# A perceiver block with a mixture of experts on one core: the gates get a tile of their own, the small groups' PSUM banks trade places, and three groups' folds move to the end

## The chip, the core and the metric

The kernel runs on one core of one Trainium2 chip. The metric is device time in microseconds; of several runs the median counts. The engines are named as in the profile: PE (TensorE's matmuls) and PEld (its weight loads), DVE (VectorE), ACT (ScalarE), POOL (GpSimd) and SP (SyncE, here the queue that issues the weights' DMAs). A `q` behind a name stands for the engine's sequencer, which waits, branches and issues.

## The reference

Three layers act on x, 8 x 64 tokens of 512 numbers, in float32: cross attention over a context of 8 x 1601 rows, a causal linear attention with a dense MLP, and a mixture of eight experts. The change lies in the third:

```python
router_logits = x @ w_router                       # x: the 512 normalized tokens
top_w, top_i = jax.lax.top_k(router_logits, K)     # K = 2
top_w = jax.nn.softmax(top_w)
gating = jnp.zeros((t, e)).at[jnp.arange(t)[:, None], top_i].add(top_w)
for ei in range(e):                                # 8 experts
    hmid = jax.nn.silu(x @ w0[ei]) * (x @ w1[ei])  # 512 -> 1024
    out = out + gating[:, ei:ei + 1] * (hmid @ wo[ei])
```

The result is added to the input of the layer.

## The kernel before

**Stages.** The span goes through cross attention (to about 164 us), linear attention (its first products begin at 129), the MLP (from 287), the routing (about 380 to 411 us) and the experts (411 us to the end). All weights come through one ring of 12 tiles that SP fills in a fixed order (`stream`, `need`, L117 to L208), six tiles ahead; a tile is issued when the matmuls that used its place are done. The order of each engine's instructions is the order of the program (a manual schedule, L95); semaphores are set by the framework from the tiles that instructions touch.

**Routing.** For each of four tiles of 128 tokens the kernel normalizes the rows into `mn` (L868, 512 columns of values and 8 of gates for each tile), writes the rows to a table in DRAM, `mn_dram` (`write`, L901), picks two experts for each token (`choose`, L933) and ranks the tokens of each expert (`rank_tile`, `tabulate`). The gates are computed last (L1102 to L1114) straight into `mn[:, :, D:]`, and a DMA on ACT's queue copies them to the last 8 columns of `mn_dram` (L1115). Then `banks.close()` and `mid.close()` (L1121, L1122) give back the PSUM banks and the SBUF pools of the middle of the kernel, `mn`'s among them (`mlp`, L814). The new pools, `pse` for PSUM and `moe2` for SBUF, are laid over them. The pool `moe` (L101) stays open from beginning to end.

**PSUM in the experts' stage.** Eight banks: three "side 0" banks and one y bank for whole tiles, two "side 1" banks (`side_bank(1)`) and one y bank (`y_bank(1)`) for the branches, one for transposed rows.

**An expert.** `whole_tile` (L1215) handles the first 128 tokens of an expert: four `up` products of 512 columns (L1224), Silu on ACT and a product on DVE (`gated`, L1182), transposes (`hidden_t`, L1189), and `down` products into y (L1232). `add_rows` (L1197) multiplies y by the gate into y_sb, on ACT (L1204) or, with `by_vector`, on DVE (L1202), and POOL adds the rows to `out` with an indirect DMA (L1205). Between its parts a whole tile turns the rows of the next expert (`turn_tile`, L1162; rows of a small group go through a side 1 bank).

Tokens beyond 128 are handled in branches that are taken or skipped at run time (`few_tokens`, L1549): up to 32 more tokens by `group` (L1254), up to 96 by `three_groups` (L1318). The test for `three_groups` (L1551) stands ahead of the one for `group` (L1553). A skipped branch still adjusts each engine's semaphore to the count that the branch would have left. In this input the experts 0, 3 and 5 take `group`, expert 2 takes `three_groups`, and 1, 4, 6 and 7 take neither (L1550; for 6 and 7 one test at L1595).

`group` lays four slices of 32 columns of the array side by side: its `up` (L1278) makes two halves h, each followed by Silu (L1286) and product (L1288); `turn` (L1265) transposes a half and copies it out, on DVE for the first and on ACT for the second; `down` (L1291) sums into two banks; two copies (L1310) and a product with `fold` (L1313) add the four slices. `three_groups` does the same for three groups of 32 tokens in full width: `up` (L1332), `turn` (L1346), `down` (L1353) with the copies L1366 to L1369, and `folded` (L1371). Their order is written out by hand at L1378 to L1391. The experts end with the whole tile of expert 7, its y_sb and its scatter.

Of the kernel before, what the change touches and what calls it, by code (L numbers as in the profile page):

```python
# [15 lines left out]
F32 = mybir.dt.float32  # L16
AF = mybir.ActivationFunctionType
ALU = mybir.AluOpType
# [29 lines left out]
def perceiver_kernel(  # L48
# [816 lines left out]

    mn = mlp.tile([P, NT, D + NE], F32, tag="mn", name="mn")  # L868
    full = [P, NT, NE]
    rank = moe.tile(full, F32, name="rank")  # L870
    spot = moe.tile([P, NT, 2], mybir.dt.uint32, name="spot")
# [18 lines left out]
    def finish(t):  # L890

        nc.vector.tensor_tensor(xs[:, t, :], acc[t], xs[:, t, :], ALU.add)  # L892
        st = small.tile([P, 6], F32, tag="st", name=f"st_m_{t}")
        nc.vector.bn_stats(st, xs[:, t, :])
        mv, rstd = moments(t, st)
        nc.vector.tensor_scalar(
            mn[:, t, :D], xs[:, t, :], mv[:, 0:1], rstd, ALU.subtract, ALU.mult
        )
        write(t)

    def write(t):  # L901
        nc.scalar.dma_start(mn_dram[t * P : (t + 1) * P, :D], mn[:, t, :D])
        nc.gpsimd.dma_start(out[t * P : (t + 1) * P, :], xs[:, t, :])

    def last_chunks(t, part):
# [171 lines left out]
    nc.vector.bn_stats(st[:, 1, :], xs[:, t, halves[1]])  # L1077
    mv, rstd = moments(t, st)
    nc.vector.scalar_tensor_tensor(neg_mean, mv[:, 0:1], -1.0, rstd, ALU.mult, ALU.mult)
    nc.scalar.activation(mn[:, t, :D], xs[:, t, :], AF.Identity, bias=neg_mean, scale=rstd)  # L1080
    first_rows(2)
    logits_of(t, range(2, KC))
    choose(t)
# [23 lines left out]
    nc.vector.tensor_scalar_add(r1, e2, 1.0)  # L1107
    nc.vector.reciprocal(r1, r1)
    nc.vector.tensor_tensor(e2, e2, r1, ALU.mult)
    gating = mn[:, :, D:]  # L1110
    nc.vector.tensor_tensor(gating, hot[:, :, 0, :], r1[:, :, None].to_broadcast(full), ALU.mult)
    hot2g = moe.tile(full, F32, name="hot2g")
    nc.vector.tensor_tensor(hot2g, hot[:, :, 1, :], e2[:, :, None].to_broadcast(full), ALU.mult)
# [11 lines left out]
    if True:  # L1125
# [71 lines left out]
        def add_rows(key, y, n, side, by_vector=False):  # L1197

            _, dst, gate = slots[key]
            y_sb = moe2.tile([P, D], F32, tag=f"ysb{side}", bufs=2 - side, name=f"y_sb_{key[0]}_{key[1]}")  # L1200
            if by_vector:
                nc.vector.tensor_scalar(y_sb[:n, :], y[:n, :], gate[:n, :], None, ALU.mult)  # L1202
            else:
                nc.scalar.activation(y_sb[:n, :], y[:n, :], AF.Copy, scale=gate[:n, :])  # L1204
            nc.gpsimd.indirect_dma_start(  # L1205
                out=out,
                out_offset=bass.IndirectOffsetOnAxis(ap=dst[:n, :], axis=0),
                in_=y_sb[:n, :],
                in_offset=None,
                bounds_check=B * S + P - 1,  # L1210
                oob_is_err=True,
                compute_op=ALU.add,
            )
# [40 lines left out]
        def group(e, up_of, down_of):  # L1254


            nm = f"{e}_1"
            xg_t = turned[e, 1]


            split = "p (w n) -> p w n"
            halves = [slice(h * P, (h + 1) * P) for h in range(2)]
            hid, h_t = [], {}

            def turn(j):  # L1265
                bank = side_bank(1, f"ht_{nm}_1") if j else y_bank(1, f"ht_{nm}_0")
                nc.tensor.transpose(bank[:, :P], hid[j], ident)
                h_t[j] = moe2.tile([P, P], F32, tag="hidT1", name=f"hidT_{nm}_{j}")
                (nc.scalar.copy if j else nc.vector.tensor_copy)(h_t[j], bank[:, :P])

            for h in range(2):
                bank = side_bank(1, f"up_{nm}_{h}")
                for c in range(KC):

                    if h == 1 and c == KC - 1:
                        turn(0)
                    for q in range(NQ):
                        nc.tensor.matmul(  # L1278
                            bank[q * R : (q + 1) * R, : 2 * P].rearrange(split, w=2),
                            xg_t[c],  # L1280
                            up_of[q][:, c, :].rearrange(split, w=2)[:, :, halves[h]],
                            start=(c == 0),
                            stop=(c == KC - 1),
                        )
                act = moe2.tile([P, P], F32, tag="act1", name=f"act_{nm}_{h}")
                nc.scalar.activation(act, bank[:, :P], AF.Silu)  # L1286
                hid.append(moe2.tile([P, P], F32, tag="mid1", name=f"mid_{nm}_{h}"))
                nc.vector.tensor_tensor(hid[h], bank[:, P : 2 * P], act, ALU.mult)  # L1288
            sums = {}

            def down(j, n):  # L1291
                if j == 0:
                    sums[n] = y_bank(1, f"yq_{nm}_1") if n else side_bank(1, f"yq_{nm}_0")
                for q in range(NQ):
                    nc.tensor.matmul(
                        sums[n][q * R : (q + 1) * R, : D // 2],
                        h_t[j][:, q * R : (q + 1) * R],
                        down_of[q // 2][:, 2 * (q % 2) + j, n * D // 2 : (n + 1) * D // 2],
                        start=(j == 0),
                        stop=(j == 1),  # L1300
                    )

            down(0, 0)
            turn(1)
            down(0, 1)
            parts = []
            for n in range(2):
                down(1, n)
                parts.append(moe2.tile([P, D // 2], F32, tag="parts", name=f"parts_{nm}_{n}"))
                (nc.scalar.copy if n else nc.vector.tensor_copy)(parts[n], sums[n][:, : D // 2])  # L1310
            y = side_bank(1, f"y_{nm}")
            for n in range(2):
                nc.tensor.matmul(  # L1313
                    y[:R, n * D // 2 : (n + 1) * D // 2], fold, parts[n], start=True, stop=True
                )
            add_rows((e, 1), y, R, 1)

        def three_groups(e, up_of, down_of):  # L1318
# [32 lines left out]
                nc.vector.tensor_copy(h_t[g].rearrange("p j q -> p (j q)"), bank[:, : 2 * P])  # L1351

            def down(g):  # L1353
                bank = side_bank(1, f"yq_{nm}_{g}")
                for j in range(2):
                    for q in range(NQ):
                        nc.tensor.matmul(
# [3 lines left out]
                            start=(j == 0),  # L1361
                            stop=(j == 1),
                        )
                parts[g] = moe2.tile([P, D], F32, tag="parts3", name=f"parts_{nm}_{g}")
                if g < 2:
                    nc.scalar.copy(parts[g], bank)  # L1366
                else:
                    nc.vector.tensor_copy(parts[g][:, : D // 2], bank[:, : D // 2])
                    nc.scalar.copy(parts[g][:, D // 2 :], bank[:, D // 2 :])  # L1369

            def folded(g):  # L1371
                for n in range(2):
                    cols = slice(n * D // 2, (n + 1) * D // 2)
                    nc.tensor.matmul(
                        y[g * R : (g + 1) * R, cols], fold, parts[g][:, cols], start=True, stop=True
                    )

            up(0)  # L1378
            up(1)
# [1 line left out]
            up(2)  # L1381
            turn(1)
            down(0)
            down(1)
            turn(2)
            y = side_bank(1, f"y3_{nm}")
            folded(0)
            down(2)
            folded(1)
            folded(2)  # L1390
            add_rows((e, 1), y, REST, 1, by_vector=True)  # L1391

        if True:
# [313 lines left out]
```

## Time and profile before

| | us |
|---|---|
| three runs | 652.44, 654.95, 656.95 |
| median | 654.95 |
| the profiled execution: its own time | 652.34 |
| its span, first to last instruction | 650.2 |
| routing ends, expert 0's first `up` | 411.07 |
| `group` of expert 0 | 436.19 to 443.90 |
| `three_groups` of expert 2 | 489.98 to 510.87 |
| `group` of expert 3 | 534.73 to 542.44 |
| `group` of expert 5 | 589.02 to 596.74 |
| last y_sb, last scatter issued | 641.79, 642.76 |

The mean granted clock of TensorE is 0.995 of full speed. The page gives the busy time and share of each engine, the chain of work that ended last, and the costliest groups of instructions; a group's line names source line, engine, operation, output and inputs, shape and count. In an answer in order of time, a line gives start and duration in us, and in brackets how long the engine stood idle before it and what ended that. A list of waits gives who waited, for whom, us in total, times and the longest.

### The profile page before, as it was taken

Reading aid. Unit: us, or ns where it says so; the run is one execution under the profiler, and the core shown is the slowest. Engines: PE = TensorE matmul, PEld = TensorE weight load, DVE = VectorE, ACT = ScalarE, POOL = GpSimd, SP = SyncE. Lnnn points to the kernel's source line nnn. Section 1 sums busy time; section 2 is a strip of 40 time slices with the busy share of each in tenths; the row PEclk is TensorE's granted clock in tenths of the full one; section 3 lists DMA queues with packets and bytes.
Section 4 is the critical chain, followed back from the end, with each engine's and each line's share of the span. In section 5 each row is a group of like instructions: output and inputs, shape, how many; then the busy total and the mean of one; then the engine's idle time right before and its main releaser. Section 6 shows DMA issues by size and latency. Waiting matters only on the chain.

```text
span 650.2 us, 7530 instructions
## 1 busy us (share of the span) xinstructions
PE 622.0 (96%) x2956; PEld 293.3 (45%) x2956; DVE 180.8 (28%) x438; ACT 128.6 (20%) x246; POOL 62.1 (10%) x82
## 2 busy tenths in 40 slices
PE   4999999999999999999999999899999999999994
PEld 3743535343444444455444457544443444443442
DVE  4011333232316878660000035411311101011110
ACT  2241222220132123031101201311111111111110
POOL 3000000000000000050000002250102002103000
PEclk9999999999999999999999999999999999999998
DMA  8999999999521203030311222339392549496611
GB/s 325 417 423 422 424 425 422 427 426 423 219 98 34 98 1 131 1 130 0 129 64 67 81 98 106 108 94 349 123 368 46 199 204 306 185 367 191 282 18 16
DMA packets 23860, 133.99 MB, mean 206 GB/s; under 512 B 4080, under 2 KB 4080, under 8 KB 12288
## 3 DMA queue, kind: packets, MB, share of 16 engines
q1 hardware_dynamic: 19456, 124.64, 48.0%
q0 software_dynamic: 3248, 7.58, 5.3%
q10 hardware_dynamic: 1104, 1.07, 0.5%
q8 instruction: 34, 0.56, 0.3%
q14 instruction: 18, 0.15, 0.1%
HBM read 128.37 MB, written 4.91 MB: 205 GB/s over the span
## 4 chain that ended last, share of the span: by engine, by line
PE 47%; DMA 25%; issue 22%; DVE 2%; POOL 1%; POOLq 1%; ACT 0%; SPq 0%; DVEq 0%; ACTq 0%
DMA out_dram<-y_sb,dst_late 11%; DMA ctx<-in_ctx_dram 10%; PE hid L823 8%; PE mlp L844 7%; PE wk L631 4%; PE wq L631 4%; PE v L551 4%; PE wo L742 4%; PE pw L374 3%; DMA ctxT<-in_ctx_T_dram 2%; PE av L487 2%; PE sc L429 2%; PE pr_wq L647 1%; PE xo L521 1%; PE qk L673 1%
## 5 line engine op out<-in xcount | busy, mean ns | idle before, releaser
L1224 PE MATMUL up<-e_up,xgT 128*128 128x512 f32 x224 | 100.2, 595 | 2.1 <-ACTq L1550 0.8
L1224 PEld LDWEIGHTS up<-e_up,xgT 128*128 128x128 f32 x224 | 40.9, 190 | 49.7 <-issue 48.2
L1232 PE MATMUL y<-e_wo,hidT 128*128 128x512 f32 x128 | 60.7, 598 | 0.0
L823 PE MATMUL hid<-v_sb,w 128*128 128x512 f32 (+2 forms) x144 | 56.6, 545 | 0.0
L1186 DVE TENSOR_TENSOR mid<-up,act 128x256 f32<-128x256 f32 x35 | 14.8, 425 | 134.6 <-ACT act L1184 134.6
L844 PE MATMUL mlp<-w,hid_sb 128*128 128x512 f32 x112 | 51.0, 597 | 0.0
L487 PE MATMUL av<-ctx,eT 128*64 128x512 f32 x192 | 46.6, 597 | 1.0 <-DMA ctx<-in_ctx_dram 1.0
L429 PE MATMUL sc<-ctxT,pw_t 128*64 128x401 f32 (+1 forms) x256 | 47.4, 501 | 0.0
L823 PEld LDWEIGHTS hid<-v_sb,w 128*128 128x128 f32 x144 | 26.2, 190 | 29.1 <-issue 27.3
L1205 POOL DMA_INDIRECT out_dram<-y_sb,dst_late x12 | 18.3, 1524 | 177.7 <-ACT y_sb L1204 79.1
L1184 ACT ACTIVATE act<-up 128x256 f32<-128x256 f32 x35 | 13.4, 385 | 107.1 <-PE up L1224 97.2
L429 PEld LDWEIGHTS sc<-ctxT,pw_t 128*64 128x64 f32 x256 | 20.9, 136 | 25.4 <-issue 22.1
L838 POOL TENSOR_TENSOR xin<-xin,b_bc 128x512 f32<-128x512 f32 x4 | 5.0, 1261 | 277.0 <-DVE rstd_h L780 272.8
L1232 PEld LDWEIGHTS y<-e_wo,hidT 128*128 128x128 f32 x128 | 22.5, 190 | 19.9 <-issue 19.6
L844 PEld LDWEIGHTS mlp<-w,hid_sb 128*128 128x128 f32 x112 | 20.7, 190 | 23.5 <-issue 23.4
L742 PE MATMUL wo<-wo,a_t 128*128 128x512 f32 x64 | 29.1, 600 | 0.6 <-DVE a_t L718 0.6
L631 PE MATMUL wk<-h_t,wk 128*128 128x512 f32 x64 | 29.5, 603 | 0.0
L631 PE MATMUL wq<-h_t,wq 128*128 128x512 f32 x64 | 29.4, 602 | 0.0
L551 PE MATMUL v<-wv,h_t 128*128 128x512 f32 x64 | 28.7, 596 | 0.6 <-DVE h_t L538 0.6
L716 DVE RECIPROCAL rden<-rden 128x512 f32<-128x512 f32 x8 | 26.8, 3353 | 0.3
L892 DVE TENSOR_TENSOR xs<-mlp,xs 128x512 f32<-128x512 f32 x3 | 2.1, 692 | 86.6 <-PE mlp L844 86.6
L487 PEld LDWEIGHTS av<-ctx,eT 128*64 128x64 f32 x192 | 13.7, 136 | 27.2 <-issue 23.2
(258 smaller groups left out, 644.1 us busy)
## 6 DMA issues: line engine op xcount, KB each, us to landing
e_up<-in_L_ffn_up_dram SPq DMA_DIRECT2D x32, 1024.0 KB, 8.0
ctx<-in_ctx_dram SPq DMA_DIRECT2D x24, 1024.0 KB, 17.3
ctxT<-in_ctx_T_dram SPq DMA_DIRECT2D x24, 802.0 KB, 15.5
e_wo<-in_L_ffn_wo_dram SPq DMA_DIRECT2D x16, 1024.0 KB, 11.2
w<-in_L_attn_w_dram SPq DMA_DIRECT2D x8, 1024.0 KB, 7.0
ctxT<-in_ctx_T_dram SPq DMA_DIRECT2D x8, 796.0 KB, 16.5
tail<-in_ctx_tail_dram SPq DMA_DIRECT2D x4, 512.0 KB, 16.8
wv<-in_L_attn_wv_dram SPq DMA_DIRECT2D x2, 1024.0 KB, 17.2
```

The costliest lines, as they stand in the source:

```text
L374: nc.tensor.matmul(bank[:, : 2 * P], w_sb[:, oc, hc * P : (hc + 1) * P], p_t[:, oc, cols], start=(oc == 0), stop=(oc == KC - 1),)
L429: nc.tensor.matmul(sc[h * S : (h + 1) * S, :width], pw_t[:, c, (2 * t + h) * S : (2 * t + h + 1) * S], keys[h][:, c, :], start=(c == 0), s ...
L487: nc.tensor.matmul(av[h * S : (h + 1) * S, :], e_t[:, 4 * g + j, h * S : (h + 1) * S], rows[h][:, j, :], start=(g == 0 and j == 0), stop=F ...
L551: nc.tensor.matmul(bank, h_t[:, c, t * P : (t + 1) * P], wv_n[:, c, :], start=(c == 0), stop=(c == KC - 1))
L631: nc.tensor.matmul(bank, w[:, c, (j % 4) * P : (j % 4 + 1) * P], h_t[:, c, :], start=(c == 0), stop=(c == KC - 1),)
L716: nc.vector.reciprocal(rden, rden)
L742: nc.tensor.matmul(wo_banks[t], a_t[:, j, t * P : (t + 1) * P], wo_r[j // 4][:, j % 4, :], start=(j == 0), stop=(j == nj - 1),)
L823: nc.tensor.matmul(hid_banks[f][:, tokens], w[:, c, (f % 4) * P : (f % 4 + 1) * P], h2_t[:, c, tokens], start=(c == 0), stop=(c == KC - 1),)
L844: nc.tensor.matmul(acc[t], hid[:, t * P : (t + 1) * P], need("w2", f // 4)[:, f % 4, :], start=(f == 0), stop=(f == FF // P - 1),)
L1205: nc.gpsimd.indirect_dma_start(out=out, out_offset=bass.IndirectOffsetOnAxis(ap=dst[:n, :], axis=0), in_=y_sb[:n, :], in_offset=None, boun ...
L1224: nc.tensor.matmul(bank, xg_t[c], up_of[q][:, c, :], start=(c == 0), stop=(c == KC - 1))
L1232: nc.tensor.matmul(y, h_t[:, j, :], w[:, 2 * (q % 2) + j, :], start=(q + j == 0), stop=(q + j == NQ))
```

## The change

`mn` loses its last eight columns and the gates get a tile of their own in `moe`. For the key of the last expert's whole tile, `add_rows` does the left half of y_sb on ACT and the right half on DVE. In `group`, the first `up` goes to the y bank, and both transposes go to side banks (before, the first `up` had a side bank and the first transpose the y bank). In `three_groups`, `parts` gets three buffers; the copies stand in the written order, where parts[1] moves from ACT to DVE; `turn(2)` stands ahead of `down(1)`; y takes the y bank instead of a side bank; and the six folds follow all of `down`, first those of the left half of the columns, then those of the right.

```diff
--- before.py
+++ after.py
@@ -865,7 +865,7 @@
 
 
 
-    mn = mlp.tile([P, NT, D + NE], F32, tag="mn", name="mn")
+    mn = mlp.tile([P, NT, D], F32, tag="mn", name="mn")
     full = [P, NT, NE]
     rank = moe.tile(full, F32, name="rank")
     spot = moe.tile([P, NT, 2], mybir.dt.uint32, name="spot")
@@ -894,12 +894,12 @@
         nc.vector.bn_stats(st, xs[:, t, :])
         mv, rstd = moments(t, st)
         nc.vector.tensor_scalar(
-            mn[:, t, :D], xs[:, t, :], mv[:, 0:1], rstd, ALU.subtract, ALU.mult
+            mn[:, t, :], xs[:, t, :], mv[:, 0:1], rstd, ALU.subtract, ALU.mult
         )
         write(t)
 
     def write(t):
-        nc.scalar.dma_start(mn_dram[t * P : (t + 1) * P, :D], mn[:, t, :D])
+        nc.scalar.dma_start(mn_dram[t * P : (t + 1) * P, :D], mn[:, t, :])
         nc.gpsimd.dma_start(out[t * P : (t + 1) * P, :], xs[:, t, :])
 
     def last_chunks(t, part):
@@ -1077,7 +1077,7 @@
     nc.vector.bn_stats(st[:, 1, :], xs[:, t, halves[1]])
     mv, rstd = moments(t, st)
     nc.vector.scalar_tensor_tensor(neg_mean, mv[:, 0:1], -1.0, rstd, ALU.mult, ALU.mult)
-    nc.scalar.activation(mn[:, t, :D], xs[:, t, :], AF.Identity, bias=neg_mean, scale=rstd)
+    nc.scalar.activation(mn[:, t, :], xs[:, t, :], AF.Identity, bias=neg_mean, scale=rstd)
     first_rows(2)
     logits_of(t, range(2, KC))
     choose(t)
@@ -1107,7 +1107,7 @@
     nc.vector.tensor_scalar_add(r1, e2, 1.0)
     nc.vector.reciprocal(r1, r1)
     nc.vector.tensor_tensor(e2, e2, r1, ALU.mult)
-    gating = mn[:, :, D:]
+    gating = moe.tile(full, F32, name="gating")
     nc.vector.tensor_tensor(gating, hot[:, :, 0, :], r1[:, :, None].to_broadcast(full), ALU.mult)
     hot2g = moe.tile(full, F32, name="hot2g")
     nc.vector.tensor_tensor(hot2g, hot[:, :, 1, :], e2[:, :, None].to_broadcast(full), ALU.mult)
@@ -1198,7 +1198,10 @@
 
             _, dst, gate = slots[key]
             y_sb = moe2.tile([P, D], F32, tag=f"ysb{side}", bufs=2 - side, name=f"y_sb_{key[0]}_{key[1]}")
-            if by_vector:
+            if key == (NE - 1, 0):
+                nc.scalar.activation(y_sb[:n, : D // 2], y[:n, : D // 2], AF.Copy, scale=gate[:n, :])
+                nc.vector.tensor_scalar(y_sb[:n, D // 2 :], y[:n, D // 2 :], gate[:n, :], None, ALU.mult)
+            elif by_vector:
                 nc.vector.tensor_scalar(y_sb[:n, :], y[:n, :], gate[:n, :], None, ALU.mult)
             else:
                 nc.scalar.activation(y_sb[:n, :], y[:n, :], AF.Copy, scale=gate[:n, :])
@@ -1263,13 +1266,14 @@
             hid, h_t = [], {}
 
             def turn(j):
-                bank = side_bank(1, f"ht_{nm}_1") if j else y_bank(1, f"ht_{nm}_0")
+                bank = side_bank(1, f"ht_{nm}_{j}")
                 nc.tensor.transpose(bank[:, :P], hid[j], ident)
                 h_t[j] = moe2.tile([P, P], F32, tag="hidT1", name=f"hidT_{nm}_{j}")
                 (nc.scalar.copy if j else nc.vector.tensor_copy)(h_t[j], bank[:, :P])
 
             for h in range(2):
-                bank = side_bank(1, f"up_{nm}_{h}")
+
+                bank = side_bank(1, f"up_{nm}_1") if h else y_bank(1, f"up_{nm}_0")
                 for c in range(KC):
 
                     if h == 1 and c == KC - 1:
@@ -1351,7 +1355,7 @@
                 nc.vector.tensor_copy(h_t[g].rearrange("p j q -> p (j q)"), bank[:, : 2 * P])
 
             def down(g):
-                bank = side_bank(1, f"yq_{nm}_{g}")
+                bank = sums[g] = side_bank(1, f"yq_{nm}_{g}")
                 for j in range(2):
                     for q in range(NQ):
                         nc.tensor.matmul(
@@ -1361,19 +1365,14 @@
                             start=(j == 0),
                             stop=(j == 1),
                         )
-                parts[g] = moe2.tile([P, D], F32, tag="parts3", name=f"parts_{nm}_{g}")
-                if g < 2:
-                    nc.scalar.copy(parts[g], bank)
-                else:
-                    nc.vector.tensor_copy(parts[g][:, : D // 2], bank[:, : D // 2])
-                    nc.scalar.copy(parts[g][:, D // 2 :], bank[:, D // 2 :])
-
-            def folded(g):
-                for n in range(2):
-                    cols = slice(n * D // 2, (n + 1) * D // 2)
-                    nc.tensor.matmul(
-                        y[g * R : (g + 1) * R, cols], fold, parts[g][:, cols], start=True, stop=True
-                    )
+                parts[g] = moe2.tile([P, D], F32, tag="parts3", bufs=3, name=f"parts_{nm}_{g}")
+
+            halves = [slice(n * D // 2, (n + 1) * D // 2) for n in range(2)]
+
+            def folded(g, n):
+                nc.tensor.matmul(
+                    y[g * R : (g + 1) * R, halves[n]], fold, parts[g][:, halves[n]], start=True, stop=True
+                )
 
             up(0)
             up(1)
@@ -1381,13 +1380,17 @@
             up(2)
             turn(1)
             down(0)
+            nc.scalar.copy(parts[0], sums[0])
+            turn(2)
             down(1)
-            turn(2)
-            y = side_bank(1, f"y3_{nm}")
-            folded(0)
+            nc.vector.tensor_copy(parts[1], sums[1])
             down(2)
-            folded(1)
-            folded(2)
+            nc.vector.tensor_copy(parts[2][:, halves[0]], sums[2][:, halves[0]])
+            nc.scalar.copy(parts[2][:, halves[1]], sums[2][:, halves[1]])
+
+            y = y_bank(1, f"y3_{nm}")
+            for g, n in [(0, 0), (1, 0), (2, 0), (0, 1), (1, 1), (2, 1)]:
+                folded(g, n)
             add_rows((e, 1), y, REST, 1, by_vector=True)
 
         if True:
```

## The prediction

> **What bounds the kernel now.** I read the page first (busy time, chain), then the waits of TensorE (PE) over the experts' stage from 400 us on, then the order of time around each spot that the change touches.
>
> ```profile
> span 650.2 us, 7530 instructions
> PE 622.0 (96%) x2956; PEld 293.3 (45%) x2956; DVE 180.8 (28%) x438; ACT 128.6 (20%) x246; POOL 62.1 (10%) x82
> ```
>
> PE is busy 96% of the span, so a change that leaves the matmuls alone can win only part of the 28 us in which PE stands still, and only where PE is what stands still. The profile's chain names DMA scatters for the last third, but these hang from one PE result to the next. I follow PE. Its waits in the experts' stage (us in total, times, longest):
>
> ```profile
> PE up L1278 <- ACTq L1551: 3.2, 3, 1.3
> PE ht L1192 <- DVE mid L1186: 0.9, 1, 0.9
> PE up L1224 <- ACTq L1550: 0.8, 1, 0.8
> PE up L1224 <- PEq L1553: 0.8, 1, 0.8
> PE up L1224 <- PEq L1595: 0.3, 1, 0.3
> ```
>
> The list is short: some 3.2 us at the entry of three small groups (experts 0, 3, 5), 0.9 us once behind the first expert's Silu. The change's three named parts aim at these two and at the tail of the one three_groups branch (expert 2). All of it together is below 6 us, under 1% of the time.
>
> **Part 1, gates in their own tile: -1.08 us.** Lines of ScalarE (ACT) and PE at the start of expert 0, in order of time:
>
> ```profile
> 415.04 0.38 ACTq L1115 DMA_DIRECT2D mn_dram<-mn  x1
> 416.90 1.28 ACT L1184 ACT_TABLE_LOAD   x1 [2.96 <-DMA mn_dram<-mn]
> 418.20 0.66 ACT L1184 ACTIVATE act<-up 128x256 f32<-128x256 f32 x2
> ...
> 417.58 0.59 PE L1224 MATMUL up<-e_up,xgT_first 128*128 128x512 f32 x1
> 419.09 0.44 PE L1192 MATMUL ht<-ident,mid 128*128 128x128 f32 x2 [0.92 <-DVE mid L1186]
> ```
>
> The gates lie in mn, which belongs to the pools that mid.close() gives back (L1122). The first Silu writes into a pool laid over them, so ACT waits for the gates' own DMA to land (415.04 + 1.8), although its operand `up` has been ready since about 414.6. Then come a table load of 1.28, Silu 0.38, the product 0.42, and PE's transpose starts 1.51 after the last `up` matmul (419.09 - 417.58); elsewhere (427.75 to 428.17) it is 0.42 to 0.43. With the gates in moe, which stays open, ACT's other waits of that row (the DMA of mn's last rows, landed 412.1) are over at about 415.58. Table load to 416.87, Silu to 417.25, product to 417.72: 0.3 before PE wants it at 418.01. PE gains 419.09 - 418.01 = 1.08. A rule speaks against it: the Trainium skill, "ScalarE: Activation LUTs", What ACT_TABLE_LOAD costs, puts a switch of tables at about 2.66 us, of which 1.38 is a drain behind the 1.28. By that estimate Silu would start at 418.24, the product end at 419.08, and part 1 give nothing. The row decides: its load starts at 416.90 and its Silu at 418.20, 1.30 later. What comes next in PE's order is the transpose of the fetched rows of (1, 0) and (0, 1), at 432.05 and 432.60; their DMAs landed at 429.2 and 430.8, so 1.08 earlier they still don't wait (0.7 is left). Bounds: 0 to -1.1. The narrower mn and the new tile cost nothing: the DVE writes, the DMA count and the rows in DRAM are the same.
>
> **Part 2, the small group starts in y's bank: -2.0 us.** Queue rows of the branch line L1551, count, duration in ns, first and last start:
>
> ```profile
> L1551 DVEq EVENT_SEMAPHORE  x3: 21/21/21, 434.1 to 585.2; - x3
> L1551 PEldq EVENT_SEMAPHORE  x3: 51/51/51, 435.0 to 588.2; - x3
> L1551 ACTq EVENT_SEMAPHORE  x3: 17/17/17, 436.1 to 589.0; - x3
> ```
>
> When three_groups is skipped, each engine makes up its semaphore count. The first `up` bank (a side bank) is read by ACT inside the skipped branch, so PE must see ACT's make-up, and ACT comes to it only after its y_sb (0.69) and two branches. In y's bank, three_groups' readers are all DVE, before and after the change (xgt3, ht, now y3 through add_rows by_vector), and DVE passes at 434.1 and 585.2, 0.9 and 3.0 before PE itself. What is left is PE's own drain and branch: in expert 0 its last wait instruction of L1278 runs at 435.26 for 0.05, plus 0.02, so it could load at 435.33 and did at 436.19. So 0.86 for expert 0, 0.74 for expert 3 (533.99 against 534.73), 0.42 for expert 5 (588.60 against 589.02): 2.02. Cross-check: 3.2 less three times the 0.3 to 0.4 that PE waits where only its own drain counts (L1595: 0.3) is 2.0 to 2.3. The second `up` still meets ACT's make-up, but 1.7 us later (64 matmuls), when it is past.
>
> The banks inside the group move too. The two transposes now both use side banks: up_1, ht_0, yq_0, ht_1, y. I take the sum of two ends here. If the pool went round in turn, yq_0 would get up_1's bank and wait for that half's product, and its 8 matmuls (0.43 us), which now fill PE's wait for it (440.15 to 441.04), would come behind it: +0.43 x 3 = +1.3. If the pool hands out the bank released first, yq_0 gets ht_0's bank, free since its copy: 0. The built program of before speaks for the second: after three_groups, where y3 was taken before yq_2 but released after it, the next `up` has yq_2's bank in every expert. I take 0.
>
> **Part 3, three_groups' folds last: -0.74 us, once.** The end of the branch before:
>
> ```profile
> 508.09 2.03 PE L1374 MATMUL y<-parts,fold 128*32 128x256 f32 x8
> 508.59 0.42 DVE L1368 COPY parts<-yq 128x256 f32<-128x256 f32 x1 [2.39 <-PE yq L1357]
> 509.05 0.37 ACT L1369 COPY parts<-yq 128x256 f32<-128x256 f32 x1 [3.03 <-DVE parts L1368]
> 509.06 0.14 PEld L1374 LDWEIGHTS y<-parts,fold 128*32 128x32 f32 x2 [0.43 <-DVE parts L1368]
> ```
>
> Fold 0 (4 matmuls at 0.216, 0.69 with the step to down(2)) leaves its place before down(2). With turn(2) between down(0) and down(1), down(2) starts at 501.72 + 1.72 + 0.14 + 0.37 + 1.72 = 505.67 instead of 506.35. The DVE copy of its first half starts 2.25 later, at 507.92, ends 508.35; ACT's half follows at 508.38 to 508.75. DVE has parts[1] as well now (0.69, 506.0 to 506.7): done before. Folds of three groups write different columns of the array and run side by side, as L1278's quads do (four starts within 0.02); and a third parts buffer spares parts[2] a wait for fold 0. Folds (0) and (1) fit into the waits, and the last one, (2, 1), starts its two passes at 508.78 and 509.0 against 509.74 before. So -0.74; the drain and branch behind it (1.1 to 510.87) stay. Were the folds to run one after another, 12 x 0.216 from 507.41 would end the last start at 509.9: +0.2. Bounds +0.2 to -1.1; I take -0.74, nearest the quads.
>
> **Part 4, the last y_sb split between ACT and DVE: +0.30 us.** It lies on the path to the end: PE's last matmul, y_sb at 641.79 (0.69), the scatter at 642.76, its landing, the end. A second rule of the skill, "TensorEngine Tiling (Array Packing)", PSUM Bottleneck, says to use both engines for evacuation: halves side by side would take 0.48 instead of 0.69, -0.2. But two halves of one bank into one tile do not run side by side here:
>
> ```profile
> ACT v_sb L790 <- DVE v_sb L794: 4.3, 6, 1.9
> ACT parts L1369 <- DVE parts L1368: 3.0, 1, 3.0
> DVE v_sb L794 <- ACT v_sb L790: 2.1, 4, 0.6
> ```
>
> L1369 began 0.03 after L1368's end. In sequence: ACT half 0.37 + 0.10 for the scale (687 - 586 ns at full width) = 0.47, step 0.03, DVE half 0.43 + 0.05 = 0.48; 0.98 - 0.69 = +0.30.
>
> **Sum.** -1.08 - 2.02 - 0.74 + 0.30 = -3.5 us. Span 650.2 to 646.7; the execution's own time 652.3 (2.1 outside the span) to 648.8. The three runs have 652.4 to 657.0 with the median 654.95, 2.6 above the profiled one, so I forecast **651.4**. The weights keep their distance: each expert's last DMA lands 5 us or more before use, and its issue waits for PE, so both move together.
>
> **Rivals.**
> - *The tail and the small groups give back half* (0.2): banks go round in turn (+1.3), or ACT still gates the entry through the second bank (+1 to +2). Sum -1.5 to -2.2: 652.8 to 653.5. For it: the ring's rule is inferred from one place. Against it: that place repeats in every expert.
> - *Part 1 does nothing* (0.1): another tile of the closed pools holds ACT until 416.8. -2.4: 652.5. Against it: every other DMA of that wait landed by 412.1.
> - *Slower* (0.08): PE's code. At L1550 PE's branch took 3.3 us twice:
>
> ```profile
> L1550 PEldq COMPARE_BRANCH  x6: 87/100/3317, 431.9 to 584.7; - x6
> ```
>
>   Both are skipped branches (463.79, 561.72), while 16 KB of instructions were fetched; queued matmuls hid all but 0.45 at the first. Inside the taken branches nothing waits for code. If the changed code put such a fetch behind an entry that is drained, each costs 3.3 in the open; the change turns slower than before from two on (6.6 - 3.5 = +3.1: 658). The number of instructions hardly changes, so I give it little.
>
> **How the numbers follow.** Likeliest case 0.62, with its own range 649.5 to 653 from the parts' bounds and the runs' scatter (4.5 us between three runs, so some 1.5 on a median). The rivals lie at 652.5 to 658. Eight in ten: 648.8 to 654.8. Faster by over 1% would need 648.4 or less, about twice the sum: 0.05, from scatter. Slower by over 1% is 661.5: 0.03, four open code fetches or a disturbed chip. Within 1%, which is about what a measurement of this kernel can tell from no change: 0.92.
>
> **What would show it.** Right: ACT's table load at L1184 near 415.6 and no DMA wait on it; no ACT wait at the small group's first matmul (0.3 to 0.4 of PE's own left); the last fold near 509 less the 1.9 gained before it; the two halves of the last y_sb one behind the other, scatter 1.27 after y instead of 0.96. Wrong: PE waiting inside the small group for `mid` before yq_0, for DVE at its entry, or a branch of several us in front of a group.

## The result, and the profile after

| | before | after |
|---|---|---|
| median of 7 runs, same chip | 656.38 us (652.44 to 658.02) | 650.13 us (648.23 to 651.08) |
| profiled execution: own time, span | 652.34, 650.2 | 649.56, 647.5 |

The ratio on record is 0.9933 (95% interval 0.9906 to 0.9961), some 4.4 us: faster by 0.7%, inside the band that counts as no change. The medians lie 6.25 us apart; their quotient is 0.9905. On two more chips the ratio was 0.9932 (0.9908 to 0.9956) and 0.9922 (0.9901 to 0.9944). The two profiled spans are only 2.7 us apart. The kernel before has two heaps (clusters) of times, 3.7 us apart on the second chip, and its profiled execution belongs to the lower one; the last part of the experiments asks what makes the upper heap.

Of the profile after, first the head of the page:

```profile
span 647.5 us, 7524 instructions
PE 621.6 (96%) x2956; PEld 293.8 (45%) x2956; DVE 182.0 (28%) x440; ACT 127.8 (20%) x245; POOL 62.1 (10%) x82
```

TensorE (PE) does nearly the same work (622.0 us before), so the gain comes out of its waits. These are, in the experts' stage (in all, times, longest):

```profile
PE up L1282 <- PEq L1554: 1.3, 3, 0.4
PE ht L1270 <- DVE mid L1292: 1.0, 3, 0.3
PE up L1227 <- ACTq L1553: 1.0, 1, 1.0
PE up L1227 <- PEq L1553: 0.6, 1, 0.6
PE up L1227 <- PEq L1556: 0.5, 1, 0.5
```

The two waits at the head of the list of before are gone: 3.2 us for ScalarE (ACT) at the three small groups became 1.3 for PE's own branch, and the 0.9 behind the first Silu is not there. In order of time at the start of expert 0:

```profile
415.09 0.38 ACTq L1115 DMA_DIRECT2D mn_dram<-gating  x1
415.71 1.28 ACT L1184 ACT_TABLE_LOAD   x1 [1.71 <-DVE few L1413]
417.00 0.38 ACT L1184 ACTIVATE act<-up 128x256 f32<-128x256 f32 x1
418.06 0.38 PE L1192 MATMUL ht<-ident,mid 128*128 128x128 f32 x2
```

ACT no longer waits for the DMA of the gates; its table load starts 1.19 earlier, and PE's transpose at 418.06 instead of 419.09 (1.08 less, as the span's zero differs by 0.05). Expert 0's small group:

```profile
434.27 1.92 PE L1282 MATMUL up<-e_up,xgT 128*32 128x256 f32 x28 [0.44 <-PEq L1554]
436.43 1.92 PE L1282 MATMUL up<-e_up,xgT 128*32 128x256 f32 x28 [0.24 <-issue]
438.28 0.33 PE L1270 MATMUL ht<-ident,mid 128*128 128x128 f32 x1
```

It starts 1.92 earlier than before. But where before 56 matmul records ran in one piece, there are now two pieces of 28 with a gap that nothing in the profile releases ("issue"), so `ht` comes only 1.06 earlier. The end of `three_groups`:

```profile
506.51 1.78 PE L1373 MATMUL y<-parts,fold 128*32 128x256 f32 x12
506.76 0.43 DVE L1388 COPY parts<-yq 128x256 f32<-128x256 f32 x1 [1.02 <-PE yq L1361]
507.22 0.37 ACT L1389 COPY parts<-yq 128x256 f32<-128x256 f32 x1 [3.81 <-DVE parts L1388]
...
508.83 1.10 PE L1227 MATMUL up<-e_up,xgT 128*128 128x512 f32 x2 [0.53 <-PEq L1556]
```

The two half copies of one bank still run one behind the other. The six folds (two passes each, so twelve records) start in twos and threes within 0.01 to 0.02; only the last one starts alone. And the last y_sb:

```profile
638.93 0.47 ACT L1202 ACTIVATE y_sb<-y,xg 128x256 f32<-128x256 f32 x1 [3.01 <-PE y L1235]
639.44 0.48 DVE L1203 TENSOR_SCALAR y_sb<-y,xg 128x256 f32<-128x256 f32 x1 [4.93 <-ACT y_sb L1202]
640.20 1.55 POOL L1208 DMA_INDIRECT out_dram<-y_sb,dst_late  x1 [20.76 <-DVE y_sb L1203]
```

The halves follow each other; from y_sb's start to the scatter it takes 1.27 (0.97 before).

### The profile page after: what moved, and what is told of

Same layout as the page of the kernel before. It is cut to its first block, busy times and chain, and to the rows that moved or that the text cites. A ratio compares the mean times of both kernels' runs of the same rounds, so it can differ in the third digit from the quotient of the medians.

```text
span 647.5 us, 7524 instructions
## 1 busy us (share of the span) xinstructions
PE 621.6 (96%) x2956; PEld 293.8 (45%) x2956; DVE 182.0 (28%) x440; ACT 127.8 (20%) x245; POOL 62.1 (10%) x82
## 4 chain that ended last, share of the span: by engine, by line
PE 47%; DMA 25%; issue 22%; DVE 2%; POOL 1%; POOLq 1%; ACT 0%; SPq 0%; DVEq 0%; ACTq 0%
DMA out_dram<-y_sb,dst_late 11%; DMA ctx<-in_ctx_dram 10%; PE hid L823 8%; PE mlp L844 8%; PE wk L631 4%; PE wq L631 4%; PE v L551 4%; PE wo L742 4%; PE pw L374 3%; DMA ctxT<-in_ctx_T_dram 2%; PE av L487 2%; PE sc L429 2%; PE pr_wq L647 1%; PE xo L521 1%; PE qk L673 1%
```

## The experiments

Kernels told of together ran on the same chip. Steps between two traces are read off PE's marks (start of each kind of tile, in order).

**One part at a time**, and the kernel before once more, on a second chip. The edits are the hunks of the change:

```diff
 a_gates:  -    gating = mn[:, :, D:]
           +    gating = moe.tile(full, F32, name="gating")
 a_bank:   -                bank = side_bank(1, f"up_{nm}_{h}")
           +                bank = side_bank(1, f"up_{nm}_1") if h else y_bank(1, f"up_{nm}_0")
 a_folds:  -            folded(1)
           -            folded(2)
           +            for g, n in [(0, 0), (1, 0), (2, 0), (0, 1), (1, 1), (2, 1)]:
           +                folded(g, n)
```

> The kernel before once more, unchanged: a second profile of it, and how far apart its own executions lie. Theory (the 6.25 us between the medians is the 2.7 us between the two profiled spans plus scatter of the kernel before): ratio 1.000 with an interval of some 0.4% across, times from 652 to 658, and where this profile is a slower one than 652.3, the added time lies ahead of the changed code or in its DMAs, not at TensorE's waits at experts 0, 2, 3 and 5. Rival (the kernel before loses more at the changed places in most of its executions, and the profiled one was lucky): the gaps at the three entries, at the first Silu and at the last fold come out larger than 1.26, 1.73, 1.41, 0.92 and 0.43 us.

> Part 1 alone, the gates in a tile of their own. Theory: the table load at L1184 starts at about 415.7 instead of 416.9, TensorE's transpose behind the first expert's Silu at 418.0 instead of 419.1, and all that follows is 1.1 us earlier: -1.1 us, ratio 0.998. Rival (the gain of 1.1 is given back at a wait further on): later marks equal to before's, ratio 1.000. Rival (the excess of 6.25 us over the profiles comes from the gates' DMA into a row shared with mn): -2 or more.

> Part 2 alone, the small group's first product in y's bank. Theory: the gaps ahead of the groups of experts 0, 3 and 5 shrink by 0.8, 0.7 and 0.4 us (to 0.4, 1.0, 1.0). Theory of the instruction fetch: in expert 0 TensorE then stands still for some 0.8 us within its first 64 matmuls, with no semaphore behind it, as it did in the changed kernel, so the group ends no earlier; the whole then gains 1.1 us. Rival (the stall within the group came with the other parts, not with the earlier start): no stall, the whole gains 1.9 us, ratio 0.997.

> Part 3 alone, the folds of three groups last. Theory: from the branch's first matmul to the next expert's first one 19.7 us instead of 20.9, -1.2 us, of which 0.95 lies ahead of the last fold and 0.2 in the branch behind it. Forecast as put on record: -0.74 with nothing gained behind the last fold. Rival: the 0.2 at the exit comes from the banks of part 2, and stays at 1.13 here. In all cases the marks ahead of expert 2 stay as before.

| kernel | ratio to before (95%) | lower heap: runs, median | upper heap (a_bank: from 653.07, else from 654.61): runs, median |
|---|---|---|---|
| before, all its runs | 1 | 46, 652.91 | 29, 656.61 |
| a_before | 0.9990 (0.9972 to 1.0007) | 15, 652.77 | 7, 655.47 |
| a_gates | 0.9985 (0.9967 to 1.0003) | 16, 652.27 | 6, 655.66 |
| a_bank | 0.9964 (0.9948 to 0.9981) | 17, 651.04 | 5, 653.56 |
| a_folds | 0.9957 (0.9942 to 0.9972) | 22, 651.82 | none |

Against the lower heap of before the parts bring 0.64, 1.87 and 1.09 us, 3.6 together. For a_gates the interval over all runs includes 1, so that its gain is clear only at the transpose in the trace. a_before's profile is one of the lower heap again (7.71 us in all three groups), so it says nothing of the upper one. The traces say where the parts win. a_gates wins 1.08 at the transpose, then loses 0.17 at the rows fetched for (0, 1): they landed at 431.58 and PE was there first. It loses 0.20 inside the small group and 0.35 behind the skipped branch of expert 1 (a_before loses 0.34 there too, so this one is scatter). a_bank wins 0.83, 0.70 and 0.39 at the three entries and keeps them: its first `up` at expert 0 ran in one piece. This is the line of a_bank:

```profile
435.39 3.23 PE L1278 MATMUL up<-e_up,xgT 128*32 128x256 f32 x56 [0.44 <-PEq L1551]
```

So the early start alone makes no gap, against what I expected of this run; it takes the two parts together, 1.1 us earlier still. a_folds wins 1.02 of the branch's time, 0.93 of it up to the start of the last fold. From there to the next `up` it takes 1.05, against 1.13 before and 0.91 in the changed kernel. PE's branch at this exit (of two, the longer one; durations in ns), for before, a_folds and the changed kernel:

```profile
L1553 PEldq COMPARE_BRANCH  x2: 236/319/402, 509.7 to 510.3; - x2
L1552 PEldq COMPARE_BRANCH  x2: 228/269/310, 509.1 to 509.6; - x2
L1556 PEldq COMPARE_BRANCH  x2: 176/203/230, 507.9 to 508.5; - x2
```

So part 3 alone brings 0.08 of the 0.22 won at the exit, and part 2 alone none (1.14 in a_bank). The other 0.14 come only with the parts together; why is open, and the rival that laid the exit to part 2's banks is neither shown nor ruled out.

**A block of instructions that has not come.** In the DMA records a queue of kind "instruction" moves 16 KB pieces (view of the DMAs of the changed kernel, 433 to 437 us):

```profile
q8 instruction: 1, 0.02, 2.3%
```

The one piece in that window landed at 435.07, and PE went on at 436.43. In every trace of an unpadded kernel in which expert 0's small group stalled clearly, PE stops at the same place of its code, the 14th of its 16 first matmuls, two of a set of four done, and goes on 1.25 to 1.41 us after the landing (a_gates and c_after lose 0.20 and 0.25 there without one clear stop):

| kernel | first `up` | piece landed | goes on | group's length (7.71 without a stall) |
|---|---|---|---|---|
| a_bank | 435.39 | 435.04 | no stop | 7.71 |
| after | 434.27 | 435.07 | 436.43 | 8.56 |
| b_after | 434.32 | 436.03 | 437.32 | 9.40 |
| b_nosplit | 434.62 | 436.00 | 437.25 | 9.04 |
| c_best | 434.48 | 435.99 | 437.40 | 9.33 |

A kernel that starts at 434.3 gets to that matmul at about 435.8, a_bank at 436.9, when the piece is usable. To move the code and nothing else, I lengthened a branch that is not run, on a third chip:

```diff
-            for c in range(KC):
+            for c in list(range(KC)) * (8 if e == 0 else 1):
                 nc.tensor.transpose(
```

> The changed kernel with 28 more transposes of TensorE in expert 0's three_groups branch, which is skipped at run time; they only shift the code behind them. Theory (the stall at the 14th matmul of expert 0's small group is a block of instructions that has not come yet): the block's edge moves to another matmul, so the stall sits elsewhere in the group or goes, and the time moves by up to 0.9 us either way. Rival (a semaphore or an operand): the stall stays at the 14th matmul with 0.87 us. The stands at the skipped branches of experts 1 and 4 (1.6 and 1.2 us) move too by the theory, and stay by the rival.

The padded kernel ran 8.08 us in that group:

```profile
434.49 3.59 PE L1282 MATMUL up<-e_up,xgT 128*32 128x256 f32 x56 [0.44 <-PEq L1554]
```

The 56 records are one piece again, in 3.59 us where a_bank took 3.23. PE passed the 14th matmul without a stop and stopped some six matmuls later, for 0.2 us there and 0.37 in all. So the place of the stop follows the code, and the rival of a semaphore or an operand, which had it at the 14th matmul, falls. That PE waits for this piece rests on the times beside the landings, and here they fit less well: the piece landed at 434.95 and PE went on 1.89 later. The total did not move (653.48 us against 653.44 of the changed kernel beside it). In the padded kernel's trace the 1.3 us won here (9.40 in b_after) are lost again at expert 5, whose group took 10.76 us against 9.33. Stretches of that time, with busy us (and instructions) of PE, PEld, DVE, ACT and POOL, then the granted clock, the share of the DMA engines and their GB/s:

```profile
590.23:593.64 3.41, 1.52 (x18) 0.43 (x18) 0.58 (x2) 0.28 (x1) 2.14 (x3) 1.00 0.96 179
593.64:597.05 3.41, 3.41 (x27) 1.28 (x27) 0.42 (x1) 0.60 (x2) 0.00 (x0) 0.50 0.87 307
```

The clock fell to one half for 3.41 us, behind a stretch in which PE was busy for only 1.52. This points to the clock and not to the padding: of the six runs, two with a mean clock of 0.996 and 0.997 took 652.12 and 652.63, three with 0.992 took 653.46 to 653.93 (the last, with 0.995, 654.15). The stands at the skipped branches of experts 1 and 4 (1.63 and 0.89, beside 1.71 and 0.89) did not shift with the padding, which I had expected.

**The split of the last y_sb** was taken back in one kernel:

```diff
-            if key == (NE - 1, 0):
-                nc.scalar.activation(y_sb[:n, : D // 2], y[:n, : D // 2], AF.Copy, scale=gate[:n, :])
-                nc.vector.tensor_scalar(y_sb[:n, D // 2 :], y[:n, D // 2 :], gate[:n, :], None, ALU.mult)
-            elif by_vector:
+            if by_vector:
```

> The changed kernel once more, unchanged, for its own scatter. The times of the kernel before lie in two heaps on a second chip, 652.3 to 653.7 (three in five) and 655 to 658 (two in five); the kernel with the new fold order alone had all 22 runs within 651.6 to 652.3. Theory (what makes the upper heap is undone by the new fold order, so the changed kernel has one heap): one heap 0.5 to 1 us wide near 649.5, ratio to the median of before 0.994 to 0.995. Rival (the upper heap is the chip's, in any kernel at times): two heaps, with some tens of per cent of the runs 3 to 4 us up. TensorE standing still 0.4 to 0.9 us at the 14th matmul of expert 0's small group, until about 1.3 us after the block of instructions requested at the branch has landed, in either case.

> The changed kernel without part 4: the last y_sb in one piece on ScalarE again. Forecast of part 4: this is faster by 0.3 us, the scatter 0.96 after y_sb's start instead of 1.27, ratio to the changed kernel 0.9995. By the rule to share an evacuation between two engines: slower by 0.2. Rival (the 0.3 is swallowed by the landing of the scatter, which has other work in front of it): same end.

The changed kernel had 653.44 us (652.98 to 655.23), this one 653.04 (652.82 to 653.56). In its trace:

```profile
642.31 0.69 ACT L1204 ACTIVATE y_sb<-y,xg 128x512 f32<-128x512 f32 x1 [3.01 <-PE y L1232]
643.28 1.55 POOL L1205 DMA_INDIRECT out_dram<-y_sb,dst_late  x1 [20.45 <-ACT y_sb L1204]
```

From y_sb to scatter 0.97 against 1.27: part 4 costs 0.30 in the trace. The medians are 0.40 apart in the same direction, but the runs overlap. The changed kernel on this chip stood at 653.4 and not near 649.5: in its trace the groups of experts 3 and 5 lost 2.7 us (8.81 and 9.33 for 7.71), of which below, and expert 0's group 0.8 more than on the first chip, as its piece landed later.

**The upper heap.** All runs of the kernel before on the third chip lay between 655.6 and 660.4, so one more execution of it was profiled there.

> One more look at the kernel before, for a profile of its upper heap (655 to 658 against 652.3 to 653.7). By the theory of code blocks the added 3.5 us sit at one or two branches of TensorE, in front of which it waits for a 16 KB block; by the rival of the DMA rings they sit at waits for weights; by the rival of the clock they are spread over all matmuls. If this run is of the lower heap it tells nothing.

It took 655.61 us (span 653.5), the fastest of the upper heap on this chip; the median there is 658.16. Up to the small group of expert 3 the trace is the one of before, to 0.3 us. There it loses 0.8, and at expert 5 2.3 more, which is all of the added 3.1. Expert 5's group in this execution, PE, then ACT and VectorE (DVE):

```profile
593.32 0.33 PE L1267 MATMUL ht<-ident,mid 128*128 128x128 f32 x1
593.58 0.64 PE L1278 MATMUL up<-e_up,xgT 128*32 128x256 f32 x8
595.54 0.64 PE L1295 MATMUL yq<-e_wo,hidT 128*32 128x256 f32 x8 [1.33 <-issue]
597.28 0.33 PE L1267 MATMUL ht<-ident,mid 128*128 128x128 f32 x1 [1.10 <-DVE mid L1288]
```

```profile
595.10 0.29 DVE L1269 COPY hidT<-ht 128x128 f32<-128x128 f32 x1 [2.29 <-PE up L1278]
```

```profile
596.62 0.28 ACT L1286 ACTIVATE act<-up 128x128 f32<-128x128 f32 x1 [4.13 <-PE yq L1295]
```

PE did its transpose at 593.32. DVE, which has only to copy it, was idle for 2.29 and began at 595.10, 1.78 later; before, it was 0.37 (transpose at 592.18):

```profile
592.55 0.29 DVE L1269 COPY hidT<-ht 128x128 f32<-128x128 f32 x1 [0.88 <-PE ht L1267]
```

DVE and ACT were idle in between, and PE had only the last eight records of `up` to do. PE's semaphore counts (by which the other engines learn that a matmul is done) come late: in the records PE's counter moves at 592.14 and then not until 595.05, 2.91 later; at expert 3 it stands from 537.01 to 539.62, 2.61. In the kernel before both steps take 1.3, so the counts are 1.6 and 1.3 late here, and the second Silu of expert 5 starts 2.3 late. Both times, and not at expert 0's group, GpSimd (POOL) has just issued a scatter and is issuing the gathers for expert e+2 behind it:

```profile
592.26 1.06 POOL L1150 DMA_INDIRECT xg<-mn_dram,src_late  x1 [0.30 <-issue]
593.63 1.00 POOL L1150 DMA_INDIRECT xg<-mn_dram,src_late  x1 [0.31 <-issue]
594.93 1.03 POOL L1150 DMA_INDIRECT xg_big<-mn_dram,src_big_False  x1 [0.30 <-issue]
```

The counts move again when that scatter lands (539.14 to 539.77, 594.57 to 595.08). No 16 KB instruction piece is near at expert 5 (587.1 and 603.8; an 8 KB one at 590.83 has its like in the kernel before at 589.48), and no weights are waited for. But the kernel before, in the profile of its lower heap, issues the same gathers at the same place, 2.11 us after its group's start at 589.02, and loses nothing:

```profile
591.13 1.05 POOL L1150 DMA_INDIRECT xg<-mn_dram,src_late  x1 [0.31 <-issue]
```

So the gathers' place alone is not the cause; at most it is one condition. To test whether it is one, the gathers (and the first spare one, `fetch_big`, not shown in the cut) were put behind the small branches, in the kernel before and in the changed one without part 4, on a fourth chip:

```diff
-                if 3 <= e + 2 < NE:
-                    for i in range(2):
-                        fetch((e + 2, i), REST if i else P)
...
                 if e < NE - 2:
                     few_tokens(e, up_of, down_of)
+                if 3 <= e + 2 < NE:
+                    for i in range(2):
+                        fetch((e + 2, i), REST if i else P)
```

> The kernel before, with the gathers for expert e+2 (and the first spare one) issued behind expert e's small branches instead of ahead of them. In a slower execution of the kernel before (span 653.5 against 650.2) the added time sat in the small groups of experts 3 and 5 only: TensorE's semaphore counts came 1.1 to 2.5 us late there while these gathers ran. Theory (the gathers, or GpSimd's issuing of them, hold up the counts): both stalls go, all runs lie in one heap near the kernel before's lower one (652.3 to 653.7 on the chip where both heaps were seen), the median 1 to 5 us under the kernel before's on this chip, ratio 0.992 to 0.999. Rival (the stalls come from instruction blocks or weights): they stay at experts 3 and 5, ratio 1.000. Rival (they move into the next whole tile with the gathers): same total.

> The changed kernel without part 4 and with the gathers behind the small branches. Theory of the gathers: no late counts in the groups of experts 3 and 5 (up to 2.7 us in the changed kernel's second profile), and 0.3 from the whole y_sb: 0.3 to 3 us under the changed kernel on the same chip. Rival: 0.3 only.

> The changed kernel unchanged, as the measure for the others on this chip. Expected at the kernel before less 3 us where no counts come late, and less 4 to 6 where they do, since the kernel before lost as much or more by them.

> Part 3 alone once more on another chip, where it had one heap of times on the first one. Theory (the fold order shifts the gathers against the group so that the counts are in time): one heap again, the median 1 us under the lower heap of the kernel before. Rival (chance of that chip): two heaps or only the upper one, as the kernel before on this chip less 1 us.

| kernel | runs on the fourth chip | group of expert 3 | group of expert 5 |
|---|---|---|---|
| before | 657.40 us (655.43 to 661.13) | not profiled here; b_look 8.51 | b_look 9.97 |
| c_folds | 655.59 (654.23 to 656.81) | 8.52 | 9.97 |
| c_after | 651.61 (651.22 to 653.05) | 8.84 | 9.34 |
| c_before_later | six at 652.38 to 653.00, six at 656.07 to 658.09 | 7.71 | 7.71 |
| c_best | 649.50 (649.02 to 650.24) | 7.71 | 7.71 |

With the gathers moved, all four groups have 7.71, the length without any stall. DVE's copy at expert 5 in c_best, 0.37 behind the transpose at 590.00:

```profile
590.37 0.29 DVE L1269 COPY hidT<-ht 128x128 f32<-128x128 f32 x1 [0.86 <-PE ht L1267]
```

The scatter ahead of them stayed where it was. So on this chip the late counts need the gathers beside the group: that is shown, as far as two profiles with moved gathers against two without (c_after, c_folds) go. Whether it is GpSimd's issuing or the transfers themselves that hold the counts up was not separated. What else it takes is open: all six profiles of the third and fourth chip with the gathers in the old place show late counts, and none of the six of the first and second chip does, though the kernel before, the changed kernel and part 3 alone are in both groups. c_folds shows that the fold order does not keep the counts in time: here it has b_look's losses to 0.01, so the single heap of a_folds on the second chip has another reason.

c_before_later has half of its runs at 656 to 658 all the same, and its profile (own time 657.52) shows another reason. At the exit of `three_groups` the branch of PE's sequencer (count, then shortest, median and longest in ns) took 2.53 us, and the whole tile behind it ran slowly:

```profile
L1553 PEldq COMPARE_BRANCH  x2: 240/1384/2529, 509.9 to 510.4; - x2
```

```profile
513.07 10.06 PE L1224 MATMUL up<-e_up,xgT 128*128 128x512 f32 x16 [2.89 <-issue]
```

Stretches of that time, with the columns as above:

```profile
510.00:513.00 3.00, 0.18 (x1) 0.00 (x0) 0.75 (x1) 0.00 (x0) 1.46 (x1) 0.87 0.53 145
513.00:516.00 3.00, 2.93 (x4) 1.42 (x5) 0.00 (x0) 0.00 (x0) 2.12 (x2) 0.50 1.02 371
516.00:519.00 3.00, 3.00 (x4) 1.11 (x4) 0.00 (x0) 0.00 (x0) 0.00 (x0) 0.50 1.04 332
519.00:522.00 3.00, 3.00 (x8) 1.33 (x7) 0.42 (x1) 0.39 (x1) 0.00 (x0) 1.00 1.02 384
```

Its piece of instructions was asked for at 510.57 (landed 511.49); before, at 507.31, 3 us ahead of the exit. PE stood from 510.2 to 513.1, the clock fell to 0.50 at 512.19 and came back at 519.02: matmuls every 0.855 us instead of 0.43. Some 5.1 us are lost: 2.1 at the branch and 3.0 by the clock. The rule nearest to this is in the Trainium skill, "TensorE: Matmul & The Clock Gate", What's actually happening: half rate after an idle window of about 3.4 us, full rate after a busy one. The stretches at half rate are two such windows long here (6.83) and one in the padded kernel (3.41), but the clock fell after 2.0 us of idleness here, and there after idle times of 0.69 and 1.20; in the 3.4 us before each fall PE was busy for 1.4 and 1.5. So the measured falls need less idleness than the rule says. Why the piece was asked for so late stays open; in c_best, where it was asked for at 505.74, nothing of the kind happens. So moving the gathers is worth it with the changed kernel, where all five runs lie below c_after's lowest (0.3 of the 2.1 us belongs to part 4), and half lost with the one before.

That second reason bears on the heaps of the second chip. With the gathers moved, the kernel before on the fourth chip has the same two heaps (652.4 to 653.0, 656.1 to 658.1) that it has on the second chip with the gathers in place (652.3 to 653.7, 654.6 to 658.3). On the second chip 24 of its 29 upper runs, from 656.3 on, have a mean clock of 0.992 to 0.995, the lower 46 of 0.995 to 0.998; b_look has 0.997 and the profiled c_before_later 0.992. And a_folds, which changes the exit of `three_groups`, has no upper heap there. This speaks for a stand at that exit, with the half rate behind it, rather than for late counts; as no upper run of the second chip was profiled, it is not shown.

## Why the prediction was right, and where it was not

- **Part 1** (-1.08): right at the spot it named, with the table load at 415.71 (forecast 415.58) and Silu 1.29 behind it; the dearer table switch is again not there. The step "1.08 earlier they still don't wait (0.7 is left)" failed in some executions: the gathered rows landed at 431.08 in the changed kernel (no wait), 431.58 in a_gates (0.17 waited), 431.79 in b_nosplit (0.34).
- **Part 2** (-2.02): the entries gave 0.83, 0.71 and 0.39 (0.86, 0.74 and 0.42 forecast), and the inference on the banks' order held, 7.71 us for the groups of experts 3 and 5 before and after. The step that failed is "Inside the taken branches nothing waits for code": expert 0's gain was eaten by the instruction piece, 0.85 of 0.83. The rival "slower" had the right resource with the wrong price, 3.3 us taken from skipped branches; inside the group it is what is left of the landing.
- **Part 3** (-0.74): mechanism right, size too small; the branch from its first transpose to the next `up` is 1.16 shorter (20.89 to 19.73). The DVE copy of the last bank begins 17.66 after the first transpose, not 17.94: `down(2)` follows `down(1)` at once, without the restart behind fold 0 that the row of before had in it; that is argued from the two rows, not tried. Counted from the first transpose, the last fold starts 0.20 earlier than forecast. The other 0.22 came from the exit, which I held fixed: PE's branch there took 0.40, now 0.23.
- **Part 4** (+0.30): right, in the trace (1.27 for 0.97) and by taking it back. Two engines for one bank do not halve the time here.
- **The sum**: -3.5 forecast, 2.7 between the spans. The difference is expert 0 (0.85) and PE's skipped branches of experts 1 and 4 (0.19 and 0.29 more, about what they differ by between two profiles of the kernel before: 0.34 and 0.19), less the 0.42 of part 3.
- **From span to median**: the profiled execution lay 2.6 below its median, and I carried that over. It was the term that failed, by 2.0: the changed kernel's median is 0.57 above its profiled run. The 2.6 was no scatter around one value: most runs of the kernel before lie in an upper heap that its profile does not show. What makes that heap on the first chip is open, as none of its upper runs was profiled there: late counts cost 3.1 us in b_look on the third chip, the stand at `three_groups`' exit with the half rate 5.1 in c_before_later on the fourth. That the forecast 651.4 lies 1.3 from 650.13 owes something to these two errors working against each other.

Open: why the changed kernel on the first chip showed no late counts (7.71 twice), and on the third and fourth 2.7 us of them. The moment of the gathers is not what differs: they start 2.50 us after expert 5's group does in all three. The times of the kernel before on the third and fourth chip, up to 661 us, are not explained either beyond the 655.6 of b_look.

## What to carry to other kernels

When medians and profiles disagree, profile the same kernel again until both heaps have a trace, and compare group by group: the lengths of identical pieces of work (7.71 here) show at once where one stands. Compare the mean clock of each run too: a short stretch at half rate shows there when no profile caught it. A gain won by starting a branch earlier holds only as far as its instructions have arrived; ask when the piece was requested, not only which semaphore comes last. And try gathers behind such a group of short pieces of work, not beside it: beside it they went with losses of 2.7 to 3.1 us on two of four chips, and behind it the group had its full speed in both profiles.

## What the runs showed of the hardware that was not expected

- Behind the skipped branches of experts 1 and 4 PE goes on 1.71 to 1.95 us after its 16 KB instruction piece has landed, in all 14 traces. Within expert 0's branch it was 1.25 to 1.41 in four traces, and 1.89 in the padded kernel.
- PE's semaphore counts came up to 2.3 us late while indirect DMAs ran (expert 5 in b_look), with its matmuls ahead of them issued in time.
- The clock fell to one half after 2.0 us without a matmul and stayed there for 6.83 (c_before_later), and after idle times of 0.69 and 1.20 for 3.41 (b_pad8); idle times of 1.33 and 1.10 at expert 5 in b_look did not bring it down.
